# Router logits of two batches at once, with the expert vectors as weights on column groups, and routing by pairs of batches

## The chip, the core and the metric

The kernel runs on one core of one Trainium2 chip; all data is float32. The metric is the device time of one execution in microseconds (us). Engines of the core: TensorE (PE in the profile; its weight loads are listed apart as PEld), VectorE (DVE), ScalarE (ACT), GpSimd (POOL) and SyncE (SP, which only issues transfers).

## The reference, cut to what matters

One decoder layer over 16 batches of 256 tokens of width 256, in three blocks with a normalisation (mean and deviation) behind each: a gated recurrence, a cross-attention of the tokens over a context of 77 rows and themselves (8 heads of width 128), and a mixture of 8 experts.

```python
x = layernorm(x + recurrence(x))                 # 16 states per token, a scan over 256 steps
x = layernorm(x + cross_attention(ctx, x))       # keys: 77 of ctx + 256 of x = 333
x = layernorm(x + experts(x))

def experts(x):
    dot = x.reshape(4096, 256) @ expert_embeddings.T         # 4096 x 8 logits
    vals, idx = top_k(dot, 2)                                # two experts a token
    weights = softmax(dot at idx, -inf elsewhere)
    ones = weights > 0
    cap_ones = where(cumsum(ones, axis=0) <= 512, ones, 0)   # 512 places an expert, in token order
    vals, index = top_k((weights * cap_ones).T, 512)         # each expert's tokens
    inter = relu(x[index] @ first_linear.T)
    out = inter @ second_linear.T * vals
    return zeros.at[index].add(out)
```

The counting runs in token order, so a batch is placed after all batches before it: a running count by expert (`carry`) goes from batch to batch.

## The kernel before

**The loop.** The main part is a loop over 16 batches x 8 heads. Every head has the same work on TensorE: keys `pk` and queries `pq` (`head_kq`), the scores `s` (`head_softmax`), the turn of the normalised weights `pa`, `pb` (`head_turn`), and the product with the values `po` (`head_out`, two heads later). In between, each head carries steps of other stages, by a schedule written out by hand: `at(b, h, f)` puts a step behind `head_kq` of batch b, head h, and `behind(b, h, f)` puts it behind the turn of the head before. A rule of the order: within one pass the order is `head_kq`, the steps of `at`, `head_out` of two heads ago, `head_softmax`, `head_turn` of one head ago, the steps of `behind`. Each engine executes its instructions in the order in which the program gives them, unless a tile waits for a buffer; an `issue_after` pushes instructions behind a named one.

**What rides on batch b for the batch before.** While batch b's heads run, batch b-1 is finished:

- heads 1 to 3: the output projection, in two parts. `project_sums` makes sums of head outputs (`osum`, `ot`; the last of them on VectorE, L708 and L709) and `project_pairs` multiplies them (`pw`, L729). Part 0 also makes `xb`, the tokens plus a bias, on GpSimd (L722), with an `issue_after` on the power `normed[b + 2]` of a later batch's normalisation. Part 1 ends in the second normalisation, whose powers GpSimd computes (L136).
- head 5: `turn_tokens` turns the 256 finished tokens into `x2` (256 features in two blocks of 128 partitions by 256 tokens), one buffer.
- head 6: `score_experts` (L819) multiplies: for each of the two blocks of tokens and of features one instruction with 128 columns of `x2` as weights and the 8 expert vectors `emb_s` as the moving side, four products, each of which is two records of the trace (`pl`, eight records in all); each writes 8 columns. A copy takes the logits to `lg`.
- head 6: `choose`, some twenty small VectorE operations on tiles of 128 x 2 x 8: the first and second maximum, their one-hot masks, the two weights, and `on`, the mask of chosen experts. The columns behind each token (`xs[:, :, 256:262]`: weights, token number, slots) are written here and in `dispatch`, the token numbers by GpSimd.
- head 7: `dispatch`: `pc` (L886, L887), two products of `on` with a triangle and with ones, which count tokens by expert; then the places (`base`, `cum`, `place`) and the row indices `sidx` (L918); then four indirect transfers (L921, issued by GpSimd) scatter the 2 x 128 token rows with two choices each to `xg` in device memory.
- head 7: `settle`, the normalisation of the tokens as they are without any expert, and a store of them.

**What rides on batch b for the next one.** For an even next batch, made in pairs, the recurrence: `rec_state` at (3, 0), (7, 0), (11, 0) takes four batches at once. Each of the four fills 32 rows of one result tile: `px` (L360, 32 weight columns, 256 wide, four blocks of the inner width for each of the four column groups, 32 records) and `sg` (L372), then `zb` on VectorE (L380), exponentials on ScalarE, a product `pp` with a permutation (L385), and the scan on VectorE; `rec_add` (`py`, L404) one head later needs the scan. `rec_out` normalises and writes `xs`. For every next batch `prep_norm` makes the third normalisation: GpSimd's chain `again` gives `rlz` (L136), and `zl` on VectorE (L500) applies it; `prep_keys`, `prep_sums`, `prep_values` follow.

**Softmax.** `nm` (L604, the row maximum), two exponentials into `p`, `rs` (L610, the reciprocal of the sum), then `pn` = `p` times `rs` into a tile of its own (L613); the turn reads `pn`.

**The tail.** After the last head, batch 15's projection, routing and scatters, then the experts in slots, one behind the other: rows of an expert's tokens are read (`xe`), turned (`turn_rows`, `pe`, L1143), multiplied by the first matrix (`pi`, L1158) and by the second one (`pf`, L1183, four tiles of 128 tokens). In the loop over the slots, `turn_rows` of the next slot stands ahead of `second_product` of this one, except for slot 0.

```python
            at(b, 5 - early, turn_tokens, b - 1)
            at(b, 6 - early, score_experts, b - 1)
            at(b, 6 - early, choose, b - 1)
            at(b, 7 - early, dispatch, b - 1)
            at(b, 7, settle, b - 1)
```

(`early` is 2 in the last batch and 0 elsewhere.)

## Time and profile before

| what | value |
|---|---|
| median of three runs | 1172.68 us (1170.93 to 1177.48) |
| the profiled execution: its time | 1174.61 us |
| its span, first to last instruction | 1172.9 us |
| mean granted clock of TensorE | 0.998 |
| scatters of the router, GpSimd L921 | 64 of 1.03 us each |
| count of logit records `pl` | 8 a batch, in 16 batches |
| value products `po`, the largest group of TensorE | 768 of 0.38 us, 190.9 us in all |
| largest group of VectorE, the row maximum `nm` | 128 of 0.85 us, 108.3 us in all |

The profile is of one execution. Its time is that of the device, and its span goes from the first to the last instruction; 1.7 us lie around the span. "Busy" is the time in which an engine executed something; matmuls are pipelined and their ends are modelled, so on TensorE the distance from one start to the next one is a better price than the listed duration. In a row of a group, `out<-in` names the tiles, `x8` the number of instructions put together, and what stands in brackets is the idle time ahead of it and who ended it. In a slice of 40 equal parts each is 29.3 us long:

```profile
PE   7999999999999999999999999999999999999996
...
POOL 2211243113311331232213322232122212144454
PEclk9999999999999999999999999999999999999999
```

TensorE is short of 9 tenths in the first slice and in the last one alone, and at full granted clock all along. GpSimd is at 1 to 4 tenths up to the tail.

### The profile page before, as it was taken

The page shows a single profiled execution, that of the slowest core. Times are in us where ns is not written, and L with a number is a line of the kernel's source. Part 1 is how long each engine was busy: PE and PEld are TensorE (multiplying, and loading weights), DVE is VectorE, ACT ScalarE, POOL GpSimd, SP SyncE. Part 2 cuts the span into 40 slices and gives each one's busy share as a digit, 9 for nine tenths or more (in the row PEclk, how much of TensorE's full clock was granted, in tenths as well). Part 3 has the DMA queues.
Part 4 walks back from the last instruction along what each step waited for, and adds up shares of the span by engine and source line. Part 5 has one row for each costly group of instructions (what it writes and reads, how often), then busy time and mean ns, then how long its engine had stood idle before and what let it go on. Part 6 is the DMA issues. An engine that isn't in the chain of part 4 may idle for free. (4 is left out here: it accounts for less than half of the span.)

```text
span 1172.9 us, 16419 instructions
## 1 busy us (share of the span) xinstructions
PE 1140.7 (97%) x5436; PEld 833.5 (71%) x5436; DVE 812.1 (69%) x2367; ACT 494.5 (42%) x1298; POOL 321.2 (27%) x564
## 2 busy tenths in 40 slices
PE   7999999999999999999999999999999999999996
PEld 3465676777787877677777777687877778876664
DVE  6655878686757776876678767766576664665665
ACT  3344444443444444444445444444444443523331
POOL 2211243113311331232213322232122212144454
PEclk9999999999999999999999999999999999999999
DMA  7740101001000010000000100000001000045752
GB/s 253 217 144 33 35 22 37 12 28 39 24 25 17 28 37 22 27 29 19 15 10 24 37 14 10 14 19 14 10 14 46 24 10 12 21 162 137 180 161 87
DMA packets 47149, 60.67 MB, mean 52 GB/s; under 512 B 7941, under 2 KB 37102, under 8 KB 47064
## 3 DMA queue, kind: packets, MB, share of 16 engines
q1 hardware_dynamic: 39686, 50.31, 13.5%
q0 software_dynamic: 6048, 9.22, 3.1%
q8 instruction: 43, 0.70, 0.3%
q14 instruction: 42, 0.34, 0.1%
q10 hardware_dynamic: 1330, 0.10, 0.1%
HBM read 36.33 MB, written 30.78 MB: 57 GB/s over the span
## 5 line engine op out<-in xcount | busy, mean ns | idle before, releaser
L639 PE MATMUL po<-ptt,v 128*128 128x256 f32 (+1 forms) x768 | 190.9, 382 | 1.6 <-DVE rs L610 1.6
L639 PEld LDWEIGHTS po<-ptt,v 128*128 128x128 f32 (+1 forms) x768 | 141.5, 190 | 53.1 <-issue 35.5
L587 PE MATMUL pk<-kvt,wkv_s 128*128 128x333 f32 x512 | 165.3, 444 | 0.0
L602 PE MATMUL s<-kt,qt 128*128 128x333 f32 x512 | 164.3, 442 | 0.0
L604 DVE TENSOR_REDUCE nm<-s 128x2 f32<-128x666 f32 x128 | 108.3, 846 | 54.3 <-PE s L602 54.1
L608 ACT ACTIVATE p<-s,nm 128x333 f32<-128x333 f32 x256 | 135.4, 535 | 22.6 <-DVE nm L604 21.9
L647 ACT ACTIVATE ot<-po,bkv_s 128x256 f32<-128x256 f32 x128 | 60.8, 475 | 172.0 <-PE po L639 171.0
L592 PE MATMUL pq<-kvt,wq_s 128*128 128x256 f32 x512 | 131.2, 379 | 0.0
L587 PEld LDWEIGHTS pk<-kvt,wkv_s 128*128 128x128 f32 x512 | 91.1, 191 | 45.9 <-issue 23.2
L602 PEld LDWEIGHTS s<-kt,qt 128*128 128x128 f32 x512 | 96.5, 189 | 30.9 <-issue 0.5
L592 PEld LDWEIGHTS pq<-kvt,wq_s 128*128 128x128 f32 x512 | 96.7, 189 | 30.5 <-issue 0.5
L628 ACT COPY ptt<-pb 77x256 f32<-77x256 f32 x128 | 47.2, 369 | 163.1 <-PE pb L625 163.1
L613 DVE TENSOR_SCALAR pn<-p,rs 128x333 f32<-128x333 f32 x256 | 100.8, 429 | 3.3
L921 POOL DMA_INDIRECT xg<-xs,sidx x64 | 65.6, 1025 | 89.2 <-DVE sidx L918 58.5
L627 DVE COPY ptt<-pa 128x512 f32<-128x512 f32 x128 | 87.2, 682 | 0.6 <-PE pa L625 0.6
L625 PEld LDWEIGHTS pa<-ident,pn 128*128 128x128 f32 x512 | 63.9, 141 | 29.3
L589 ACT ACTIVATE kt<-pk,bkv_s 128x333 f32<-128x333 f32 x128 | 68.9, 538 | 24.6 <-PE pk L587 23.8
L625 PE MATMUL pa<-ident,pn 128*128 128x128 f32 x512 | 76.8, 273 | 0.0
L339 DVE SCALAR_TENSOR_TENSOR cv<-hp,cw,cv 128x512 f32<-128x512 f32 (+1 forms) x108 | 73.9, 691 | 1.4
L594 ACT ACTIVATE qt<-pq,bqs 128x256 f32<-128x256 f32 x128 | 61.0, 477 | 18.8 <-PE pq L592 14.9
L324 PE MATMUL ph<-xT,inw 128*128 128x512 f32 (+1 forms) x144 | 63.4, 570 | 5.0 <-DMA inw<-in_in_wT 4.9
L1183 PE MATMUL pf<-w,it 128*128 128x256 f32 x272 | 61.3, 381 | 2.7 <-ACT ye L1193 1.5
(254 smaller groups left out, 1826.8 us busy)
## 6 DMA issues: line engine op xcount, KB each, us to landing
v<-vc SPq DMA_DIRECT2D x16, 308.0 KB
xg<-zero SPq DMA_DIRECT2D x34, 131.0 KB
xe<-xg SPq DMA_DIRECT2D x8, 524.0 KB
xt<-in_x_in SPq DMA_DIRECT2D x16, 256.0 KB
out<-o SPq DMA_DIRECT2D x16, 256.0 KB
w<-in_w1T SPq DMA_DIRECT2D x8, 512.0 KB
w<-in_w2T SPq DMA_DIRECT2D x8, 512.0 KB
oe<-ye SPq DMA_DIRECT2D x15, 256.0 KB
```

Of the source, the lines that this page charges most:

```text
L339: V.scalar_tensor_tensor(cv, hp[:, :, k : k + S], cw[:, c, k : k + 1], cv, ALU.mult, ALU.add)
L587: T.matmul(pk[:, 0:J], lhsT=wkv_s[:, k, f], rhs=kvt[:, k, :], start=(k == 0), stop=(k == DC - 1))
L589: A.activation(kt, pk[:, 0:J], AF.Identity, bias=bkv_s[:, h : h + 1])
L592: T.matmul(pq[:, 0:S], lhsT=wq_s[:, k, f], rhs=kvt[:, k, 0:S], start=(k == 0), stop=(k == DC - 1))
L602: T.matmul(s[:, ic, 0:J], lhsT=qt[:, ic * P : (ic + 1) * P], rhs=kt, start=True, stop=True)
L604: V.tensor_reduce(nm, s[:, :, 0:J], AX.X, ALU.max, negate=True)
L608: A.activation(p[:, ic, :], s[:, ic, 0:J], AF.Exp, bias=nm[:, ic : ic + 1], accum_out=sm[:, ic : ic + 1])
L613: V.tensor_scalar(pn[:, ic, :], p[:, ic, :], rs[:, ic : ic + 1], None, ALU.mult)
L625: T.transpose(dst[0:jn, c0 : c0 + P], pn[:, ic, j0 : j0 + jn], ident)
L627: turned = V.tensor_copy(ptt[:, 0:2, :], pt01.rearrange("p (j i) -> p j i", j=2))
L639: T.matmul(po[:, 0:S], lhsT=vs[b][0:jn, jc, h * DH : (h + 1) * DH], rhs=ptt[0:jn, jc, :], start=(jc == 0), stop=(jc == 2),)
L921: dma = G.indirect_dma_start(out=xg[:, :], out_offset=bass.IndirectOffsetOnAxis(ap=sidx[:, t, c : c + 1], axis=0), in_=xs[b][:, t, :], in_ ...
```

## The change

Fourteen of sixteen batches, 0 to 13, are now routed in pairs (0, 1), (2, 3), ... (12, 13). Batches 14 and 15 are routed singly as before.

- **Logits.** The tokens of both batches stay turned in `x2` (now two buffers). At an even batch b, head 6, `score_pair(b - 2)` uses the expert vectors as weights, padded with zeros to 32 columns, and the 256 tokens as the moving side: four products, one for each batch and each half of the features, each to a column group of its own, so to 32 of the 128 rows of one result tile. ScalarE copies it out as `lt`. The two halves of the features are not yet summed. `turn_logits`, behind head 6's turn, multiplies `lt` (as weights, 128 tokens at a time) by `sel`, a constant mask of 128 x 16 that adds the two halves and sorts by batch and expert: 16 columns a block of tokens. A copy brings them to `lg`.
- **Routing.** `choose(b - 2, 2)` stands behind head 6 and `dispatch(b - 2, 2)` behind head 7, on tiles of 128 x 4 x 8, one chain for two batches; tags that had two buffers have one. What follows each token is written to a small tile `know`, and ScalarE copies it behind the tokens, one copy a batch. `pc` is one pair of products with 32 columns.
- **Scatters.** `dispatch` scatters the first batch's four; `scatter_second`, in the next, odd batch (3 to 13) behind head 1 and with an `issue_after` on `normed` of a later batch, the second batch's four. The last pair (12, 13) scatters all at once.
- **The recurrence.** `rec_state` is cut: `px`, `sg`, `zb` and the exponentials stay, and `rec_scan` with `pp` and the scan goes to a new place, `amid`, between `head_out` and `head_softmax` of the same head.
- **Softmax.** The weights are normalised in place; `p` has three buffers.
- **The tail.** In slot 1 one tile of `second_product` goes ahead of `turn_rows(2)`.
- **Small ones.** `yl` and the two context ends use the buffer of `osum`; one of the context's value tiles moves with `x2`; an early Tanh on two columns; six buffers of `xs` for five.

```diff
-    xpool = ctx.enter_context(tc.tile_pool(name="x", bufs=5))
+    xpool = ctx.enter_context(tc.tile_pool(name="x", bufs=6))
...
-    emb_s = wpool.tile([P, DC, E], F32, tag="emb", name="emb_s")
+    emb_s = wpool.tile([P, DC, 32], F32, tag="emb", name="emb_s")
+    sel = wpool.tile([P, 2, E], F32, tag="sel", name="sel")
...
+    A.activation(small.tile([P, 2], F32, tag="warm", bufs=1, name="warm"), nhalf, AF.Tanh)
...
+        G.memset(emb_s[:, :, E:], 0.0)
+        id5 = ident.rearrange("p (i k s) -> p i k s", k=DC, s=32)
+        V.tensor_tensor(sel, id5[:, :, 0, 0:E], id5[:, :, 1, 0:E], ALU.add)
...
         A.activation(dec[R], dec[R], AF.Exp, scale=-1.0)
+        scans[first] = R, rows, members, sg, zb, dec
+        if first == 0:
+            rec_scan(first)
+    def rec_scan(first):
+        R, rows, members, sg, zb, dec = scans.pop(first)
         pp = bank(f"pp{first}")
...
-        p = b2.tile([P, 2, J], F32, tag="p", name=f"p{b}_{h}")
+        p = b2.tile([P, 2, J], F32, tag="p", bufs=3, name=f"p{b}_{h}")
...
-            V.tensor_scalar(pn[:, ic, :], p[:, ic, :], rs[:, ic : ic + 1], None, ALU.mult)
+            V.tensor_scalar(p[:, ic, :], p[:, ic, :], rs[:, ic : ic + 1], None, ALU.mult)
...
-        x2s[b] = b1.tile([P, DC, S], F32, tag="x2", name=f"x2{b}")
+        x2s[b] = b2.tile([P, DC, S], F32, tag="x2", name=f"x2{b}")
...
+    def score_pair(b):
+        pl = bank(f"pl{b}")
+        for k in range(DC):
+            for i in range(2):
+                r = 32 * (DC * i + k)
+                T.matmul(pl[r : r + 32, 0:S], lhsT=emb_s[:, k, :], rhs=x2s[b + i][:, k, :], start=True, stop=True)
+        del x2s[b], x2s[b + 1]
+        logits[b] = lt = b1.tile([P, S], F32, tag="lt", name=f"lt{b}")
+        A.copy(lt, pl[:, 0:S])
+    def turn_logits(b):
+        lt = logits.pop(b)
+        pt = bank(f"plt{b}")
+        for t in range(GT):
+            T.matmul(
+                pt[:, t * 2 * E : (t + 1) * 2 * E],
+                lhsT=lt[:, t * P : (t + 1) * P],
+                rhs=sel.rearrange("p i e -> p (i e)"),
+                start=True,
+                stop=True,
+            )
+        lgs[b] = small.tile([P, 2 * GT, E], F32, tag="lg", bufs=1, name=f"lg{b}")
+        V.tensor_copy(
+            lgs[b].rearrange("p (i t) e -> p t i e", t=GT),
+            pt[:, 0 : 2 * GT * E].rearrange("p (t i e) -> p t i e", i=2, e=E),
+        )
...
-        for i in range(GT):
-            G.tensor_scalar(x[:, i, D + 2 : D + 3], tok1, float(b * S + i * P), 1.0, ALU.add, ALU.mult)
+        x = small.tile([P, 2 * GT, DX - D], F32, tag="know", bufs=1, name=f"know{b}")[:, 0:TT, :]
+        for i in range(TT):
+            G.tensor_scalar(x[:, i, 2:3], tok1, float(b * S + i * P), 1.0, ALU.add, ALU.mult)
...
-        T.matmul(pc[:, 0 : GT * E], lhsT=tri, rhs=onf, start=True, stop=True)
-        T.matmul(pc[:, GT * E : 2 * GT * E], lhsT=ones, rhs=onf, start=True, stop=True)
+        T.matmul(pc[:, 0 : TT * E], lhsT=tri, rhs=onf, start=True, stop=True)
+        T.matmul(pc[:, TT * E : 2 * TT * E], lhsT=ones, rhs=onf, start=True, stop=True)
...
-        for t in range(GT):
+        for i in range(n):
+            A.copy(xs[b + i][:, :, D:], x[:, i * GT : (i + 1) * GT, :])
+        scatter(b, sidx, range(GT if b + 4 < B else TT))
+        sidxs[b] = sidx
+    def scatter_second(b):
+        with tc.issue_after(normed[b + 4].ins):
+            scatter(b, sidxs[b], range(GT, 2 * GT))
+    def scatter(b, sidx, tiles):
+        for t in tiles:
             for c in range(2):
                 dma = G.indirect_dma_start(
...
+    def amid(b, h, f, *args):
+        mid_steps[b, h].append((f, args))
...
-            at(b, 6 - early, score_experts, b - 1)
-            at(b, 6 - early, choose, b - 1)
-            at(b, 7 - early, dispatch, b - 1)
+            if b == B - 1:
+                at(b, 6 - early, score_experts, b - 1)
+                at(b, 6 - early, choose, b - 1, 1)
+                at(b, 7 - early, dispatch, b - 1, 1)
+            elif b % 2 == 0:
+                at(b, 6, score_pair, b - 2)
+                behind(b, 6, turn_logits, b - 2)
+                behind(b, 6, choose, b - 2, 2)
+                behind(b, 7, dispatch, b - 2, 2)
+            if b % 2 == 1 and 2 < b < B - 1:
+                behind(b, 1, scatter_second, b - 3)
...
                 at(b, 0, rec_state, nb, nb + 3)
+                amid(b, 0, rec_scan, nb)
...
         if i >= 2:
             head_out(*heads[i - 2])
+        if i < len(heads):
+            for f, args in mid_steps[heads[i]]:
+                f(*args)
...
-            if e > 0:
-                turn_rows(e + 1)
-        y = second_product(e, it)
+        tiles = list(range(SLOTS[e][2]))
+        ahead = 1 if e == 1 else 0
+        if ahead:
+            second_product(e, it, tiles[:ahead])
+        if 0 < e < LAST:
+            turn_rows(e + 1)
+        y = second_product(e, it, tiles[ahead:])
```

## The prediction

> **What bounds the kernel now.** I read the page first: TensorE is the bound.
>
> ```profile
> PE 1140.7 (97%) x5436; PEld 833.5 (71%) x5436; DVE 812.1 (69%) x2367; ACT 494.5 (42%) x1298; POOL 321.2 (27%) x564
> ```
>
> An instruction taken off TensorE is therefore worth its time, and one taken off VectorE is worth nothing unless TensorE waits for it. So the second view is who TensorE waited for (total us, times, longest).
>
> ```profile
> PE pp L385 <- issue: 3.9, 3, 1.3
> PE po L639 <- DVE rs L610: 1.6, 1, 1.6
> PE pe L1143 <- DMA xe<-xg: 1.6, 1, 1.6
> ```
>
> The first and third row are waits that the change reaches for; the second it leaves alone. Third, the timeline of TensorE where batch 3 is routed (start, us, then the group; a row's price is the distance to the next row's start).
>
> ```profile
> 367.28 0.95 PE L819 MATMUL pl<-emb_s,x 128*128 128x8 f32 x8
> 368.09 1.10 PE L552 MATMUL pv<-wsum,tsum 128*128 128x512 f32 x2
> ...
> 374.95 0.37 PE L886 MATMUL pc<-on,tri 128*128 128x16 f32 x2
> 375.17 0.37 PE L887 MATMUL pc<-on,ones 128*128 128x16 f32 x2
> 375.39 1.96 PE L324 MATMUL ph<-xT,inw 128*128 128x512 f32 x4
> ```
>
> The logits take 0.81 us and the two count products 0.44, although they write 8 and 16 columns. The matmuls behind run 0.08 over their usual time (1.10 for two `pv`, 1.02 elsewhere). One batch costs 0.89 + 0.52 = 1.41.
>
> **Off TensorE: logits and counts by pairs.** Fourteen batches are routed by pairs, two as before. A pair costs 2.82 now. Afterwards it has one pair of count products (four instructions, 0.52), one turn of the same form (128 weight columns, 16 written: 0.52), and eight instructions of 32 weight columns by 256 on four column groups. This last form the trace shows in the recurrence, at 262.98 us:
>
> ```profile
> 262.98 1.93 PE L360 MATMUL px<-hs,xpw 128*32 128x256 f32 x32
> 264.73 0.61 PE L372 MATMUL sg<-sums,half 128*32 128x256 f32 x8
> 265.27 0.70 PE L639 MATMUL po<-ptt,v 128*128 128x256 f32 x2
> 267.31 0.70 PE L385 MATMUL pp<-zb,perm 128*128 128x256 f32 x2 [1.34 <-issue]
> 267.85 1.03 PE L639 MATMUL po<-ptt,v 128*128 128x256 f32 x4
> 268.72 1.28 PE L602 MATMUL s<-kt,qt 128*128 128x333 f32 x4
> ```
>
> and on VectorE, whose `zb` reads `px`:
>
> ```profile
> 266.77 0.48 DVE L380 TENSOR_SCALAR zb<-px,xpb 128x256 f32<-128x256 f32 x1 [2.62 <-PE po L639]
> ```
>
> Forty of them are issued in 265.27 - 262.98 = 2.29 us, 0.057 each, against 0.216 for the same width on the whole array (1.73 us for eight `pf` of L1183). But `zb` starts at 266.77, 1.86 after the end that is modelled for `px` (264.91): by its reader, 32 took 3.79, 0.118 each. Eight cost 0.46 by the issue, 0.95 by the reader, 1.73 if nothing overlapped. Entering and leaving the form costs 0.1 each (four `pq` before `px` take 0.96 to the next start, 0.86 before `pc`; two `po` behind show 0.70, not 0.60). The pair then costs 1.70, 2.19 or 2.97; the gain over seven pairs is 7.8, 4.4 or a loss of 1.1. I take the middle of the first two, **-6.1**: the matmuls behind did start on time, but the wait at `pp` may hide what was still running. All three ends stay for the range.
>
> A rule speaks against this edit. "TensorEngine Tiling (Array Packing)" of the Trainium skill, section Performance Considerations, says that a matmul has some 60 cycles of overhead, so that free size 1 costs what 60 costs, and warns against tiling for a dimension that is already small. An estimate by that page (60 cycles at the 2.4 GHz of "TensorE: Matmul & The Clock Gate") gives 0.025 us for each old logit product, 0.4 a pair, and the sum would be 8.5 us worse. The rows have 0.10 each, with their 128-column weight loads, so the measurement decides for the edit.
>
> **VectorE.** Each pair runs one chain of some 36 small operations for two, on 32 instead of 16 elements, at about 0.2 us each in both forms (0.17 in the rows of 16). That saves about 25 us of VectorE and is worth 0 directly: no routing operation of VectorE stands among TensorE's longest waits. The in-place softmax, the third buffer of `p`, the early Tanh (one table load at 5.26, as before) and the moved constants cost nothing; the idle time of ScalarE (42% busy) covers its seven copies of 128x256 (0.37 each, as the 77x256 copy of L628) and sixteen narrow ones. Without that cover they would cost about 5 us.
>
> **`pp` moved behind `po`.** At three places (batches 3, 7, 11) four `po` instructions go ahead of `pp`: 268.72 - 267.85 = 0.87 saved if TensorE was idle, 0 if it was still finishing `px`. I take half, **-1.3** (0 to -2.6). What is late next is the scan: it now stands behind a row maximum and a copy (0.76 + 0.68) on VectorE, and `py` needs it. Its slack now is 272.57 - 271.43 = 1.14, so about 0.3 each, **+1.0** (0 to 3.5).
>
> **The late pair chain at the same three places.** `pc` now stands ahead of `px`, behind `pq` of the next batch's head 0, and its input `on` stands behind `rs` of the last head. `rs` is at 263.26 and `pq` ends its issue at 262.98; with `on` and its landing `pc` can start about 0.5 after TensorE asks for it: **+1.5** (0 to 2). Behind it stand `px` and everything else.
>
> **One product of expert slot 1 ahead of the turn.** Eight `pf` (1.73 us) fill the wait of 1.64 for the rows of `xe`: **-1.6** (0 to -1.6). The turned rows still have 1.73 of `pf` to cover their eviction.
>
> **The scatters in two parts.** The built order on GpSimd is: first four scatters, four token operations, `ra`, second four, `xb`, and only then `uz`, `u2z`, `u3z`, `rlz`, which `zl` waits for. On VectorE `zl` stands ahead of L708, whose result the second half of `pw` needs. These six odd batches (3 to 13) now look like batch 3:
>
> ```profile
> 265.94 0.97 POOL L921 DMA_INDIRECT xg<-xs,sidx  x1 [0.30 <-issue]
> 267.22 0.98 POOL L921 DMA_INDIRECT xg<-xs,sidx  x1 [0.30 <-issue]
> 277.12 0.72 POOL L136 TENSOR_TENSOR ra<-va,nhalf 128x2 f32<-128x2 f32 x1 [8.93 <-DVE va L147]
> 277.83 1.37 POOL L722 TENSOR_TENSOR xb<-xs,bo_s 128x256 f32<-128x256 f32 x2
> ...
> 280.05 1.07 POOL L136 TENSOR_TENSOR rlz<-u3z,nhalf 128x2 f32<-128x2 f32 x1
> ```
>
> ```profile
> 281.15 0.35 DVE L500 TENSOR_SCALAR zl<-xs,rlz 128x256 f32<-128x256 f32 x1 [0.52 <-POOL rlz L136]
> ...
> 282.28 0.69 DVE L708 TENSOR_TENSOR ot<-osum,ot 128x512 f32<-128x512 f32 x1
> ```
>
> ```profile
> 286.67 1.05 PE L729 MATMUL pw<-wosum,ot 128*128 128x128 f32 x8
> ```
>
> A scatter takes 1.28 of GpSimd (265.94 to 267.22), four 5.1. They push `rlz` from 281.12 to 286.2; two `zl` (0.65) and L708 (0.69) end at 287.6, where TensorE wants it at 286.67: a wait of about 1.0. Batches 5, 9 and 13 have a second one: the first four scatters wait for the later chain, and with the token operations (four, some 1.1) and a sum (1.3) they end about 0.4 after `ra` is due. 6 x 1.0 + 3 x 0.4 = **+7.2** (0 if `zl` is not in the way, 12 if it is 2.0 each time). The old scatters at the end of every batch cost TensorE nothing, so removing those saves nothing.
>
> **Sum.** -6.1 - 1.3 + 1.0 + 1.5 - 1.6 + 7.2 = +0.7. The profiled execution had a span of 1172.9 and a time of 1174.6, so it would come to 1175.3; it lies 1.9 above the median of the runs, 1172.7, and on the median's footing this is **1173.4**: no change that can be told.
>
> **Rivals.** *The second scatters stay hidden* (chance 0.25): -6.1 - 1.3 + 1.0 + 1.5 - 1.6 = -6.5, 1166.2. For it: 5.5 us lie between the first `rlz` and the second half of `pw`. Against: `zl` and L708 use those up by the built order. *GpSimd becomes the bound of every odd batch* (0.22), the slower one: the place is `ra` behind the first four scatters. It decides once `sidx` comes so late that they end after `ra` is due (in batch 5, after 393.45, which is `sidx` later than about 387). From there each us counts at `pw`'s first half as well; at 2.5 a batch it is 15 in place of 7.2, +8.5, 1181.2. For it: the pair's chain comes a head later. Against: batches 3, 7 and 11 have 5 us of room. *The column groups do not overlap* (0.05): +1.1 for -6.1, +7.9, 1180.6. The issue of `px` speaks against it, its reader half for it.
>
> **How the numbers follow.** About 0.5%, 5.9 us, is what a measurement of this kernel can tell from no change. The forecast holds 0.48 (its own range 1168 to 1178), faster by more 0.25, slower by more 0.27. To leave out no more than 2 in 10 the range takes in most of both sides: low is 1165 (the full issue rate, 1.7 better, with the hidden scatters), high 1181 (GpSimd late).
>
> **What would show it.** In the changed trace: `pl` in rows of 128x256 with about 0.06 between starts and `lt` copied 0.5 us after the last; TensorE's wait list with `pw <- DVE` at odd batches from 3 to 13, some 1 us each, and none in even ones; `pc` waiting for `on` at three places; no wait of `pe` for `xe`; `pp` at under 3.9. I am wrong if `pw` shows no waits (then 1166) or if `ra` is late by over a us in each odd batch.

## The result, and the profile after

| | before | after |
|---|---|---|
| median of 20 runs each | 1172.74 us (1170.61 to 1177.65) | 1169.95 us (1166.52 to 1172.19) |
| ratio of the medians, 95% interval | | 0.9969 [0.9959, 0.9978] |
| the profiled execution: time, span | 1174.61, 1172.9 us | 1172.19, 1170.5 us |
| start to the first `s` | 51.41 | 52.80 |
| batch 0 | 82.59 | 82.89 |
| the loop, batch 1 head 0 to batch 15 head 7 | 883.63 | 879.39 |
| from there to the end (the tail) | 155.27 | 155.39 |

The kernel became 0.3% faster. That is clear of the interval of its measurement, although it is less than the 0.5% which the prediction took for the least that can be told; 1173.4, no change, had been forecast. The last four rows are distances between the starts of `s` (the scores) in the two traces. The loop is what can be compared: a second profile of the changed kernel, on chip 13, had it at 879.37. Start and tail move by some microseconds from one execution to the next (50.6 to 54.8 and 149.8 to 157.3 in the profiles of this study), so most of what follows is read from the loop. It lost 4.24 us.

From the page of the kernel after, the busy times and the row of GpSimd in 40 slices:

```profile
PE 1136.3 (97%) x5380; PEld 822.2 (70%) x5380; DVE 782.1 (67%) x2144; ACT 497.1 (42%) x1315; POOL 318.0 (27%) x565
...
POOL 3201241114210530242015302340142014144454
```

TensorE has 56 matmuls and 4.4 us of work less, VectorE 30.0 us less (the prediction had about 25), and the time moved by 2.4 in the profiles. GpSimd has the same work, but in heaps: slices of 4 and 5 tenths beside slices of 0, where it lay between 1 and 4 before, and nowhere at 0. The heaps are the odd batches with eight scatters.

Who TensorE waited for, after (total us, times, longest):

```profile
PE pw L745 <- DVE ot L724: 3.5, 6, 1.3
...
PE pw L745 <- DVE ot L721: 1.9, 3, 0.7
PE pi L1239 <- issue: 1.7, 1, 1.7
...
PE pc L936 <- DVE on L926: 1.6, 3, 0.5
...
PE pe L1224 <- DMA xe<-xg: 0.3, 1, 0.3
```

`pw` and `pc` wait where they were said to (the longest of the three waits for L721, 0.7, is at batch 1 and stood in the kernel before too). `pe` has almost no wait left, but `pi`, behind it, has a new one of the same length. And a line is missing: before, `pp <- issue` stood there with 3.9, three times 1.3.

The timeline of the kernel after at the same place (batch 3, head 0), TensorE and then VectorE:

```profile
263.46 0.38 PE L936 MATMUL pc<-on,tri 128*128 128x32 f32 x2 [0.54 <-DVE on L926]
...
264.00 1.93 PE L368 MATMUL px<-hs,xpw 128*32 128x256 f32 x32
265.75 0.61 PE L380 MATMUL sg<-sums,half 128*32 128x256 f32 x8
266.29 1.56 PE L655 MATMUL po<-ptt,v 128*128 128x256 f32 x6
267.69 0.60 PE L402 MATMUL pp<-zb,perm 128*128 128x256 f32 x2
```

```profile
266.16 0.35 DVE L969 SCALAR_TENSOR_TENSOR sidx<-into,oobs,know 128x4 int32<-128x4 f32 x2
266.43 0.48 DVE L388 TENSOR_SCALAR zb<-px,xpb 128x256 f32<-128x256 f32 x1
```

`zb` starts 2.43 after the first `px`, and directly behind `sidx`, so it was VectorE that kept it. Before, the same `zb` started 3.79 after `px` with VectorE idle for 2.62 us. The matmuls are the same 32 records. Something that made `px` look slow is gone; whether that is the place of `pp`, the experiments have to tell.

Step by step, from the starts of `s` head by head (after minus before):

| step | forecast | measured |
|---|---|---|
| logits and counts by pairs, seven pairs | -6.1 | -7.9: 1.34 to 1.41 less in each odd batch and 0.13 to 0.27 less in each even one at heads 6 and 7, 0.45 more for `pc` in the head behind; so a pair costs some 1.69 in place of 2.82 |
| wait of `pp` at batches 3, 7, 11, and the later `py` | -1.3 + 1.0 | -4.6 and 0 |
| `pc` waits for `on` | +1.5 | +1.6 |
| scatters in two parts, `pw` waits | +7.2 | +6.85: batch 3 0.47, 5 2.43, 7 0.44, 9 2.41, 11 0.43, 13 0.67 |
| one product ahead in slot 1 (tail) | -1.6 | +0.5 up to the first `pi` of slot 2 |

The four rows of the loop give -4.05, against -4.24 measured; the rest is in batch 1 (0.10 more at its first head, 0.23 less at its last).

### The profile page after: what moved, and what is told of

Its sections match the earlier page's. It is cut to its first block, busy times and chain, and to the rows that moved or that the text cites. A ratio compares the mean times of both kernels' runs of the same rounds, so it can differ in the third digit from the quotient of the medians.

```text
span 1170.5 us, 16021 instructions
## 1 busy us (share of the span) xinstructions
PE 1136.3 (97%) x5380; PEld 822.2 (70%) x5380; DVE 782.1 (67%) x2144; ACT 497.1 (42%) x1315; POOL 318.0 (27%) x565
## 5 line engine op out<-in xcount | busy, mean ns | idle before, releaser
L629 DVE TENSOR_SCALAR p<-p,rs 128x333 f32<-128x333 f32 x256 | 98.3, 420 | 3.3
L641 PEld LDWEIGHTS pa<-ident,p 128*128 128x128 f32 x512 | 63.9, 141 | 29.4
L641 PE MATMUL pa<-ident,p 128*128 128x128 f32 x512 | 76.8, 273 | 0.0
```

Source lines behind the costliest of these rows:

```text
L629: V.tensor_scalar(p[:, ic, :], p[:, ic, :], rs[:, ic : ic + 1], None, ALU.mult)
L641: T.transpose(dst[0:jn, c0 : c0 + P], pn[:, ic, j0 : j0 + jn], ident)
```

## The experiments

Theories that had to be told apart: is the lost wait at `pp` worth what `pp`'s move brought, or did `px` itself become prompt, and why? Is the pair's form really cheaper than the old one? What does the late scatter cost, what the product ahead? The kernel before was run again beside each set. The runs went to several chips, and its median was 1174.3 us on chip 4, 1175.2 on chips 13 and 1, 1166.9 on chip 8 and 1166.5 on chip 6; ratios are against the runs on the same chip. "Loop" is the loop of the table above, 883.63 before and 879.39 after.

**`pp` and the scan moved alone, in the kernel before.**

```diff
+        scans[first] = R, rows, members, sg, zb, dec
+    def rec_scan(first):
+        R, rows, members, sg, zb, dec = scans.pop(first)
         pp = bank(f"pp{first}")
...
                 at(b, 0, rec_state, nb, nb + 3)
+                amid(b, 0, rec_scan, nb)
```

> The kernel before with one edit: `rec_scan` (`pp` and the scan) goes behind `head_out`, so that all six `po` stand ahead of `pp` at batches 3, 7 and 11. Theory A (an idle TensorE keeps back the signal of `px`, so the whole wait goes): `zb` starts about 2.4 us after `px` as in the changed kernel, not 3.79 as before; TensorE's wait at `pp` (3.9 in all) goes, about 1.4 a place, 4.2 in all: 0.9964 of before, about 1168.5. Theory B (as predicted: `px` is still being finished, the wait only overlaps four `po`): `zb` stays at 3.79 after `px`, some 0.4 of wait is left at each `pp`, 0.43 to 0.87 gained a place, and `py` waits 0.3: 0 to 2.6 in all, about 1172.

1175.84 us, 1.0014 [1.0001, 1.0028]; loop 884.47, 0.84 longer. Who TensorE waited for in it:

```profile
PE py L413 <- DVE ys L401: 3.1, 3, 1.0
...
PE pp L394 <- issue: 1.3, 3, 0.5
```

The move does what the prediction said, with a wrong balance: each place gains 0.89 at `pp` and loses 1.25 at `py`, where the prediction had 0.43 and 0.3 (and 0.09 to 0.14 comes back one head later). `zb` still comes 3.78 after `px`, with VectorE idle.

**The kernel after, with `pp` and the scan back in their old place.**

```diff
-        if first == 0:
-            rec_scan(first)
+        rec_scan(first)
...
-                amid(b, 0, rec_scan, nb)
```

> The changed kernel with `rec_scan` put back into `rec_state`, so that `pp` follows two `po` again; `pc` still stands ahead of `px`. Theory A: `zb` goes back to 3.8 us after `px` and `pp` waits 1.3 at three places: 4.2 slower than the changed kernel, about 1174.2. Theory B: the place of `pp` is worth 0.3 in all, about 1170.3. Theory C (it is the wait for `pc` ahead of `px` that makes `px` early, not the place of `pp`): `zb` stays at about 2.4 after `px`, `pp` waits some 0.2 at each place, 0.6 in all, about 1170.6.

1171.30 us, 0.9973 [0.9956, 0.9991]; loop 879.34, the same as after. `zb` comes 2.44 after `px`, and no wait of `pp` is among TensorE's. So the place of `pp` is worth nothing in the kernel after, and the 4.6 us come from a prompt `px`.

**The kernel after, with the old form of logits for each pair** (sixteen records with 128 weight columns, no `turn_logits`).

```diff
-                at(b, 6, score_pair, b - 2)
-                behind(b, 6, turn_logits, b - 2)
+                at(b, 6, score_both, b - 2)
```

> The changed kernel with the logits of a pair in the form of before: tokens as weights, 8 columns written, sixteen records a pair, no column groups, no turn, no copy to `lt`. Everything else by pairs. Theory A (column groups overlap at their issue rate, as the changed trace shows: the step at head 6 costs 0.77 and the turn 0.44): a pair of logits costs 1.62 + 0.16 in place of 1.21, 0.57 more, 7 pairs: 4.0 slower than the changed kernel, about 1174.0. Theory B (they cost by the rate that the reader of `px` showed, 0.95 + 0.1 + 0.52): 1.78 in place of 1.57, 1.5 slower, about 1171.4. In both `on` comes earlier and `pc` waits less at batches 3, 7 and 11, up to 1.5 to be taken off.

1174.98 us, 0.9999 [0.9989, 1.001]; loop 882.0, 2.6 longer than after. Logits in the kernel after, then in this one (TensorE and the copies):

```profile
247.99 0.64 PE L854 MATMUL pl<-x,emb_s 128*32 128x256 f32 x8
248.56 1.13 PE L569 MATMUL pv<-wsum,tsum 128*128 128x512 f32 x2
249.07 0.38 ACT L857 COPY lt<-pl 128x256 f32<-128x256 f32 x1
```

```profile
248.77 1.85 PE L854 MATMUL pl<-emb_s,x 128*128 128x8 f32 x16
250.47 1.10 PE L569 MATMUL pv<-wsum,tsum 128*128 128x512 f32 x2
```

Eight records on the column groups take 0.57 to the next start and are read 1.08 after the first; sixteen in the old form take 1.70. From the starts of `s` the old form costs 0.93 to 1.02 more a pair and saves the turn, 0.45; so the new form is 0.48 to 0.57 a pair better, 3.7 over seven, of which this run gets some 1.1 back because the counts come earlier and `pc` needn't wait. Here `px` stands directly behind `pq`, as in the kernel before, and `zb` is still prompt (2.00 after `px`): so it is not the `pc` between `pq` and `px` that made it so.

**The scatters beside `px` taken away, in the kernel before.** The four scatters of batches 1, 5 and 9 get their indices from a copy that is made behind `zb`; nothing else is changed.

```diff
+        if b not in (1, 5, 9):
+            scatter(b)
+    def scatter_late(b):
+        late = small.tile([P, GT, 2], I32, tag="late_idx", bufs=1, name=f"late_idx{b}")
+        with tc.issue_after(zbs[b + 3].ins):
+            V.tensor_copy(late, sidxs[b])
+        sidxs[b] = late
+        scatter(b)
...
                 at(b, 0, rec_state, nb, nb + 3)
+                behind(b, 0, scatter_late, b - 2)
```

> The kernel before, with the four scatters of batches 1, 5 and 9 held back until `zb` of the recurrence is done (a copy of their indices on VectorE behind `zb`, 0.16 us, is what they wait for); no other edit, `pp` stays where it was. Theory D (scatters that GpSimd issues while the forty column-group products run are what makes `px` late: in before they start at 263.24 and 504.41, 0.26 and 0.25 after `px`; in the changed kernel and its variants none runs there and `px` is signalled 0.04 after its end): `zb` starts about 2.0 after `px` instead of 3.8, the wait of 1.3 at `pp` goes at three places: 3.9 to 4.5 faster than before, 0.9964. Theory E (the cause is another difference, such as where the tiles lie): `zb` stays at 3.8 after `px`, 0 to 0.5.

1169.71 us, 0.995 [0.9932, 0.9969]; loop 878.48, 5.15 shorter than before: 1.73, 1.66 and 1.71 at batches 3, 7 and 11. Its timeline at batch 3, TensorE, VectorE and GpSimd:

```profile
265.88 1.93 PE L360 MATMUL px<-hs,xpw 128*32 128x256 f32 x32
...
267.88 0.48 DVE L380 TENSOR_SCALAR zb<-px,xpb 128x256 f32<-128x256 f32 x1 [0.83 <-PE px L360]
...
268.71 0.59 PE L385 MATMUL pp<-zb,perm 128*128 128x256 f32 x2
...
268.73 1.12 POOL L937 DMA_INDIRECT xg<-xs,late_idx  x1 [5.94 <-DVE late_idx L929]
```

`zb` comes 2.00 after `px`, at the end that is modelled for it, and `pp` waits for nothing. This one edit, which takes no work from any engine, gains as much as the whole change; its loop, 878.48, is even 0.9 shorter than that of the kernel after, so everything else in the change together costs 0.9 in the loop.

**More scatters beside `px`, in the kernel after.** Four more at the same three places, to rows that nothing reads (work that is added to the kernel).

```diff
+        where = small.tile([P, 4], I32, tag="where", bufs=1, name=f"where{b}")
+        with tc.issue_after(on_ins[b].ins):
+            V.tensor_copy(where, rows_i[:, b : b + 4])
+            for t in range(4):
+                dma = G.indirect_dma_start(
+                    out=nowhere[:, :],
...
                 behind(b, 7, dispatch, b - 2, 2)
+                if b in (2, 6, 10):
+                    behind(b, 7, scatter_more, b - 2)
```

> The changed kernel with four more scatters on GpSimd at batches 3, 7 and 11, of the token columns of a finished pair to rows that nobody reads, issued some 0.3 us after the start of `px`. Theory D: the signal of `px` is late again, by about 1.8, and `zb` starts some 3.8 after `px` and not 2.4 to 2.7; `pp`, which has four more `po` ahead of it than in before, waits 0.4, and `py` about 1.0 for the scan as in the run with `pp` moved alone; 1.2 to 1.5 a place, 4 in all. The real first scatters come 5 us later, which the 2.9 to 5 us up to `ra` hide at these batches or miss by up to 1. Theory E: `px` stays at 0.04, and only the late scatters can cost, 0 to 3 in all.

1192.40 us, 1.0147 [1.0129, 1.0166]; loop 897.12, 17.7 longer than after (3.9, 6.7 and 7.2 at the three places). At batch 7:

```profile
508.29 1.93 PE L368 MATMUL px<-hs,xpw 128*32 128x256 f32 x32
508.93 1.13 POOL L986 DMA_INDIRECT nowhere<-xs,where  x1 [5.20 <-DVE base L942]
...
513.35 0.48 DVE L388 TENSOR_SCALAR zb<-px,xpb 128x256 f32<-128x256 f32 x1 [2.29 <-PE po L655]
513.89 0.46 PEld L402 LDWEIGHTS pp<-zb,perm 128*128 128x128 f32 x2 [2.14 <-DVE zb L388]
```

The same `px` is now read 5.06 after its start, with VectorE idle for 2.29 and TensorE waiting for the answer. The direction was expected, the size wasn't: other matmuls' results (`po`, `pp`) are late as well, and at batches 7 and 11 the granted clock then stood at 0.50 for 3.4 us, behind idle stretches of TensorE of 1.74 and 3.47; at batch 3, where the run lost least, it did not fall.

**Which part of a scatter does it?** In the kernel after, at the same three places, seven elementwise operations of 128x256 on GpSimd in one run, and eight plain transfers of 128 KB issued by SyncE in another (added work in both).

```diff
+            G.tensor_scalar(junk, xs[b][:, t % 2, 0:D], tick[:, 0:1], 1.0, ALU.mult, ALU.mult)
```

```diff
+            nc.sync.dma_start(nowhere[r : r + P, :], rows_)
```

> The changed kernel with seven elementwise operations of 128x256 on GpSimd beside `px` at batches 3, 7 and 11 (their results are read by nobody), where k11 had four scatters. If GpSimd's being busy is what delays the signals, `px` is signalled 1 to 2 us after its end and `zb` starts 3.5 or more after `px`, as in k11. If it is the transfers or their indirect issue, the signal stays at 0.04 and `zb` at 2.4 to 2.7. The real scatters come later by some 5 us, up to 2 in all.

> The changed kernel with eight plain transfers of 128 rows of 1 KB from the on-chip memory to rows that nobody reads, issued by SyncE beside `px` at batches 3, 7 and 11: as many bytes as eight scatters without GpSimd. If moving the rows is what delays the signals, `px` is signalled 1 us late or more. If it is the indirect issue on GpSimd, the signal stays at 0.04 and `zb` at 2.4 to 2.7 after `px`: no change of time.

1171.54 and 1171.22 us, one execution each, on chip 1; loops 879.76 and 879.49 against 879.39. The end of `px` is signalled within 0.05 us of the modelled end in both, as without them; `zb` comes 2.85 and 2.0 to 2.1 after `px` (2.85 because VectorE is busy with `sidx`). So neither these operations on GpSimd nor this plain traffic to device memory does it, on a chip where signals near scatters are late. What in an indirect scatter does is open.

**The second scatters held behind the last power of the chain (`rlz`).**

```diff
-        with tc.issue_after(normed[b + 4].ins):
+        with tc.issue_after(zpower[b + 4].ins):
...
-                behind(b, 1, scatter_second, b - 3)
+                behind(b, 4, scatter_second, b - 3)
```

(`zpower` names the instruction that writes `rlz`.)

> The changed kernel with the second four scatters of a pair pushed behind `rlz` on GpSimd. Theory A (they stand ahead of `rlz`, and `zl` holds L724 back on VectorE): the waits of `pw` part 2 go (0.45, 1.55, 0.44, 1.55, 0.43 and 0.67 at batches 3 to 13, 5.1 in all), those of part 1 at batches 5 and 9 (0.86 each, from the first four) stay: about 1164.9. Rival (GpSimd's 5.1 us a pair only move to the sums `tsum` behind it, and `pv` waits in their place): no change, about 1170.

1167.11 us, 0.9933 [0.9915, 0.995]; loop 875.75, 3.64 shorter than after. Three waits of `pw` for the earlier sum (L721 in the kernel after) are left, 3.4 in all in place of 1.9: at batches 5 and 9 they became 0.7 longer, which is why the gain is 3.64 and not 5.1.

**All eight scatters behind `rlz`.** `dispatch` keeps `sidx`, and `scatter_second` issues all eight.

```diff
-        scatter(b, sidx, range(GT if b + 4 < B else TT))
+        if b + 4 >= B:
+            scatter(b, sidx, range(TT))
...
-            scatter(b, sidxs[b], range(GT, 2 * GT))
+            scatter(b, sidxs[b], range(2 * GT))
```

> The changed kernel with all eight scatters of a pair pushed behind `rlz` on GpSimd. Theory A: all waits of `pw` at odd batches go, 5.1 in part 2 and 1.7 in part 1 (batches 5 and 9), 6.9 in all: about 1163.1. Rival: 10.2 us of scatters ahead of `tsum` on GpSimd make `pv` wait for the sums at odd batches; from then on each us costs six times, and the gain over moving the second four alone (1.7) is lost.

1163.05 us, 0.9965 [0.9952, 0.9977] on chip 8; loop 873.9, 5.5 shorter than after. `pw` keeps 1.5 of its waits: 0.7 at batch 1, which the kernel before has too, and 0.4 each at batches 5 and 9. So 5.5 of the 6.85 belong to the place of the scatters. What stays at batches 5 and 9 (0.65 each from the starts of `s`) does not.

**No product ahead in slot 1.**

```diff
-        ahead = 1 if e == 1 else 0
+        ahead = 0
```

> The changed kernel without the tile of `second_product` ahead of `turn_rows(2)` in slot 1. Theory A (the step gained nothing: the wait for `xe`, 1.6, became one for `xet`, 1.7, since VectorE evicts the turned rows behind 26 small operations): the wait of `pe` comes back, that of `pi` goes, 0.1 either way, about 1170. Theory B (as predicted, a gain of 1.6): about 1171.6.

1169.92 us, 1.0026 [1.0017, 1.0036] on chip 8. `pe` waits 2.2 for its rows. Then `pe` and half of `pf` run slowly. Stretches of the tail: us from to, length, then busy time and instructions of five engines, the granted clock of TensorE, the share of the DMA engines and GB/s:

```profile
1047.00:1049.70 2.70, 0.52 (x3) 0.12 (x1) 1.27 (x6) 0.46 (x2) 2.38 (x3) 1.00 0.93 273
1049.70:1051.50 1.80, 1.76 (x9) 1.77 (x9) 1.65 (x14) 0.00 (x0) 1.06 (x2) 0.52 1.01 300
1051.50:1053.00 1.50, 1.50 (x5) 1.23 (x5) 1.47 (x13) 0.59 (x1) 1.04 (x2) 0.50 1.07 388
```

The clock fell to half for some 3 us after an idle stretch of 2.2 us. In the kernel before the wait was 1.64 and the clock stayed full. So the product ahead is worth 1.9 here (first `pi` of slot 2 at 40.7 us behind the last head, against 38.8), but by keeping the clock: from the first `pe` to that `pi` it is 6.06 here and was 4.39 in the kernel before, for the same work. Against the kernel before (38.2) it is worth nothing.

**The turned rows copied first.** The reads of the next slots' small data are held behind the copies of `xet`.

```diff
-                V.tensor_copy(xet[:, k, 0 : n * P], pt[:, 0 : n * P])
+                turned_rows[e] = V.tensor_copy(xet[:, k, 0 : n * P], pt[:, 0 : n * P])
...
+        if e == 1:
+            with tc.issue_after(turned_rows[2].ins):
+                rows[2].read(2)
```

> The changed kernel, with VectorE's copy of the turned rows of slot 2 put ahead of the small operations on the rows of slots 2 and 3 (`dw` to `to`), by their order alone. Theory A (the copy at 1053.04 is late because of them; the transposes end at 1050.4): the copy starts at about 1050.7 of the same scale, the wait of `pi` (1.7) goes: 1.7 faster than the changed kernel, about 1168.3. Rival (ScalarE's half of the copy or the small operations become late in their turn): 0 to 0.5.

1166.38 us, 0.9997 [0.9984, 1.001] on chip 8. The tail of the kernel after, and then of this one:

```profile
1049.33 1.09 PE L1224 MATMUL pe<-ident,xe 128*128 128x128 f32 x8 [0.32 <-DMA xe<-xg]
1050.26 1.89 PE L1266 MATMUL pf<-w,it 128*128 128x256 f32 x8
1053.83 5.39 PE L1239 MATMUL pi<-xet,w 128*128 128x512 f32 x12 [1.68 <-issue]
```

```profile
1049.96 1.09 PE L1226 MATMUL pe<-ident,xe 128*128 128x128 f32 x8 [0.83 <-DMA xe<-xg]
1050.89 1.89 PE L1268 MATMUL pf<-w,it 128*128 128x256 f32 x8
1052.62 3.69 PE L1241 MATMUL pi<-xet,w 128*128 128x512 f32 x8
```

After, VectorE did 26 small operations from 1050.21 on ahead of the copy `xet` (1053.04), and `pi` waited 1.68. With the copy first `pi` waits for nothing and starts at 37.5 in place of 38.8, which is 0.7 better than before.

**Both of these together,** all eight late and the copy first.

> Both mends together: all eight scatters behind `rlz`, and the copy of the turned rows first. If both theories hold the gains add, 6.9 + 1.7 below the changed kernel: about 1161.4, 0.990 of before. If either falls, what the single runs show.

On chip 8 1159.37 us, 0.9941 [0.9925, 0.9958]; loop 873.89. On chip 1 the same kernel:

> The best version (all scatters behind `rlz`, copy of the turned rows first) again. From the profiles it should stand 5.5 (scatters) + 1.4 (copy) below the changed kernel, whose ratio was 0.9957 to 0.9969: 0.990 to 0.992.

1173.31 us, 0.9986 [0.9976, 0.9995]; loop 882.68, 8.8 longer. The same place of batch 3 in the two runs, the end of the second half of `pw` and its reader on VectorE, on chip 8 and then on chip 1:

```profile
286.18 0.97 POOL L989 DMA_INDIRECT xg<-xs,sidx  x1 [0.30 <-issue]
...
286.60 1.06 PE L748 MATMUL pw<-wosum,ot 128*128 128x128 f32 x8
287.45 0.97 POOL L989 DMA_INDIRECT xg<-xs,sidx  x1 [0.30 <-issue]
287.69 0.29 DVE L765 TENSOR_TENSOR u<-u,pw 128x128 f32<-128x128 f32 x1 [2.94 <-PE pw L748]
```

```profile
288.39 0.97 POOL L989 DMA_INDIRECT xg<-xs,sidx  x1 [0.30 <-issue]
...
288.82 1.06 PE L748 MATMUL pw<-wosum,ot 128*128 128x128 f32 x8
289.67 0.97 POOL L989 DMA_INDIRECT xg<-xs,sidx  x1 [0.30 <-issue]
...
292.10 0.29 DVE L765 TENSOR_TENSOR u<-u,pw 128x128 f32<-128x128 f32 x1 [5.14 <-PE po L658]
```

The eight scatters run at the same place in both. On chip 8 VectorE reads `pw` 1.09 after the last group began, on chip 1 3.28 after. That delay reaches `ptt` and six `po` (7.0 us of waits there, at head 4 of the odd batches). So whether a scatter holds a signal back differs between the two runs of one kernel, and moving the scatters away from `px` put them beside `pw`. Each chip was used for one set of runs, so the chip and what else differed between the sets can't be told apart.

**Counts one head later** (both late, and `dispatch` behind the next head's turn).

```diff
-                behind(b, 7, dispatch, b - 2, 2)
+                behind(b + 1, 0, dispatch, b - 2, 2) if b < B - 2 else behind(b, 7, dispatch, b - 2, 2)
```

> The best version so far (all scatters behind `rlz`, copy of the turned rows first) with `dispatch` of a pair one head later, behind head 0 of the odd batch, so that `pc` no longer stands between `pq` and `px`. The waits of `pc` for `on` at batches 3, 7 and 11 (0.55 each, 1.6 in all) go: 1.6 faster than the best version if nothing else waits. Rival: the counting chain on VectorE, 11 operations, now stands among those of head 1 and holds back the sums for `pw` or the row maxima: the gain is lost, 0 to 1 slower.

1180.71 us, 1.0052 [1.0033, 1.0072] on chip 13; loop 888.64. It failed: `po` waits 5.2 for `ptt`, and `pw` 3.0. On chip 1, where signals are late too, the loop without the later count was 882.68; against that it is 6.0 longer. So of the 14.75 us that it is above the loop on chip 8 (873.89), some 8.8 go with late signals and some 6.0 with the later count (an estimate, since the runs are of different chips).

**Routing half a head earlier** (`score_pair` behind head 5's turn, the turn of the logits and `choose` at head 6), with both of the two, on chip 1; then the second scatters late with the copy first, on chip 6; then these with the earlier routing.

```diff
-                at(b, 6, score_pair, b - 2)
-                behind(b, 6, turn_logits, b - 2)
-                behind(b, 6, choose, b - 2, 2)
+                behind(b, 5, score_pair, b - 2)
+                at(b, 6, turn_logits, b - 2)
+                at(b, 6, choose, b - 2, 2)
```

> The best version (k8) with the routing of a pair half a head earlier: `score_pair` behind head 5, `turn_logits` and `choose` at head 6. `on` is then ready before `pc` wants it and the waits of `pc` at batches 3, 7 and 11 (0.55 each, 1.6 in all) go: 1.6 faster than k8. Rival: the 25 small operations of `choose` come into the way of `v` and `ptt` on VectorE in head 6, as the counting chain did in k10: slower by some us.

> The changed kernel with the second four scatters behind `rlz` (k4: 3.6 less in the main loop) and the copy of the turned rows first (k7: 1.4 less in the tail). No scatter then runs beside `px` or ahead of the reader of the second `pw`: about 5.0 below the changed kernel, 0.991 to 0.993 of before on a chip that holds signals back, 0.994 to 0.996 on one that does not (there the kernel before has no wait at `pp`, some 4.5 less).

> k15 with the routing of a pair half a head earlier (k14: 0.9 less in the main loop than k8, from `pc` that no longer waits). Expected another 0.9 below k15. Rival: the first scatters come earlier by about 0.7 and reach into `px`, whose signals are then held back at batches 3, 7 and 11: 2 to 4 slower than k15.

Earlier routing is worth 0.9 in the loop both times (881.8 against 882.68 on chip 1, 874.93 against 875.82 on chip 6): `pc` then waits for nothing. (The medians on chip 1, 1173.29 and 1173.31, don't show it.) Times: 1173.29 us, 0.9976 [0.996, 0.9992]; 1162.81 us, 0.9972 [0.9961, 0.9983], where 0.994 to 0.996 had been expected; 1161.51 us, 0.9953 [0.9939, 0.9966].

**The changed kernel again, on chip 13.**

> The changed kernel itself, beside the others on the same chip, since the kernel before took 1174.3 on one chip and 1166.9 on another, and so ratios of different calls can't be set against each other. If its gain is in the main loop (4.4 in the profiles, from batch 1 on, the same to 0.1 in every execution profiled) the ratio is 0.996 to 0.998 here too; a ratio above 1 would say that the start or the tail differ by chip.

1169.50 us, 0.9957 [0.9942, 0.9972]; loop 879.37 against 879.39.

The best ratios are 0.9933 (second scatters late, chip 4), 0.9941 (both late, copy first, chip 8) and 0.9953 (second late, copy first, earlier routing, chip 6). They come from different chips and can't be set against each other or against the 0.9957 and 0.9969 of the kernel after; the last arrangement wasn't run on a chip that holds signals, so which is best there is open.

## Why the prediction missed, step by step

**The step that failed** is the last sentence on the scatters: "The old scatters at the end of every batch cost TensorE nothing, so removing those saves nothing". Three of their sixteen sets ran beside `px`, and there they cost 4.6 to 5.1 us: this is what the kernel after gained at `pp`, and what the kernel before gains when only those scatters are held back. The forecast for the loop was +2.3 and the measurement is -4.24; of the difference 4.3 stand at `pp` and `py`, 1.8 at the pairs and 0.4 at the scatters. That the time still fell inside the forecast's own 1168 to 1178 is luck: the largest gain came from a cause that the sum put at nothing.

It could have been seen in the profile of before. The prediction priced `px` "by its reader" at 0.118 a record from the one row where `zb` is late. The trace has another `px`, at 129.29 us, with no scatter near (TensorE, then VectorE):

```profile
129.29 1.92 PE L360 MATMUL px<-hs,xpw 128*32 128x256 f32 x16
...
131.37 0.46 DVE L380 TENSOR_SCALAR zb<-px,xpb 64x256 f32<-64x256 f32 x1
```

Here the reader starts 2.08 after `px`, 0.16 behind its modelled end; at batch 3 it started 3.79 after, 1.86 behind the end. (This `px` uses two column groups and that of batch 3 four, so it is a hint and no proof.) The first scatter of batch 3 starts 0.26 behind `px`:

```profile
263.24 1.13 POOL L921 DMA_INDIRECT xg<-xs,sidx  x1 [3.35 <-DVE into L917]
```

**The pairs** (-6.1, measured -7.9): right in kind, and mis-sized by the same error. The middle of "0.46 by the issue, 0.95 by the reader" was taken; the full issue rate holds, and a pair costs 1.69, the low end of the prediction (1.70). The 1.41 of each odd batch came out as 1.34 to 1.41. The decision to trust the rows and not the estimate of 0.025 us for an old product was right: sixteen of them take 1.70 here, and going back to them costs 3.7 over seven pairs.

**`pp` behind `po`** (-1.3) **and `py`** (+1.0): in the kernel after worth 0 and 0, since nothing was late any more. Alone, in the kernel before, -2.7 and +3.75. What 0.89 saved at `pp` does to `py` was left out: TensorE comes there 0.89 sooner, so the slack of 1.14 shrinks to 0.25, and a scan that is 1.44 later costs 1.19 in place of 0.3 (1.25 measured).

**The wait of `pc`** (+1.5): 1.6, three times 0.5, as said.

**The scatters in two parts** (+7.2): 6.85. The mechanism of the wait in the second half of `pw` is in the timeline of the kernel after at batch 5, GpSimd, VectorE and TensorE:

```profile
393.83 0.72 POOL L136 TENSOR_TENSOR ra<-va,nhalf 128x2 f32<-128x2 f32 x1 [0.67 <-DVE va L147]
...
398.95 0.97 POOL L985 DMA_INDIRECT xg<-xs,sidx  x1 [0.30 <-issue]
...
402.05 0.72 POOL L136 TENSOR_TENSOR rlz<-u3z,nhalf 128x2 f32<-128x2 f32 x1
...
402.80 0.61 DVE L517 TENSOR_SCALAR zl<-xs,rlz 128x256 f32<-128x256 f32 x2 [5.28 <-POOL rlz L136]
...
403.33 0.68 DVE L724 TENSOR_TENSOR ot<-osum,ot 128x512 f32<-128x512 f32 x1
...
404.07 0.97 PEld L745 LDWEIGHTS pw<-wosum,ot 128*128 128x128 f32 x8 [1.67 <-DVE ot L724]
```

`pw` stands behind `ot`, that behind `zl`, that behind `rlz`, and `rlz` behind the last scatter. That the sum comes so close is partly luck, since the distribution differs from the forecast: 0.45 in place of 1.0 at batches 3, 7 and 11, 2.4 in place of 1.4 at 5 and 9, and 0.67 in place of 1.4 at 13. The second term, `ra` kept late by the first scatters, did not happen: at batch 5 GpSimd is idle for 0.67 ahead of `ra` and waits for `va` of VectorE. What makes the first half of `pw` wait there (0.89) is VectorE, which reaches `osum` 4.36 behind the start of `py` in place of 3.51 before; with all eight scatters moved it is 4.31. That the pair's counting chain ahead of it is the reason is likely, but not shown. Held behind `rlz`, the second scatters give back 3.64, all eight 5.5.

**The product ahead** (-1.6): +0.5, of which 0.4 is that the rows `xe` came later behind the last head in this execution; from the first `pe` to the first `pi` it is 4.50 in place of 4.39. The wait for `xe` went as said, from 1.64 to 0.32. What failed is "The turned rows still have 1.73 of `pf` to cover their eviction": 26 operations stand ahead of the eviction on VectorE, and the cover of sixteen `pf` (3.46 us) that the kernel before had behind its `pe` had been cut to eight. With the copy first the gain is 0.7.

**The rivals.** Scatters that stay hidden are ruled out by the waits, GpSimd as the bound of every odd batch too (at most 2.43, and in two batches of six), and column groups that don't overlap by the 1.69. What happened was no rival of the list: the gain of the edit came from moving work that had no visible price.

**Chips.** The late `px` of the kernel before was seen in its own profile and on chip 4 (in the run that moves `pp` alone), and on chip 13 the kernel gains by holding the scatters back. On chips 8 and 6 no signal of TensorE was late near a scatter, and there the kernel before takes 1166.5 to 1166.9 us, 7 to 9 less. The change with its tail mended (copy first) is worth nothing on chip 8 (0.9997), where its gain on the pairs (7.9) is used up by the waits that it adds (1.6 and 6.85). That the kernel before has no wait at `pp` there was not profiled; it is inferred from its time and from the late signals below, and `px` explains 4.6 to 5.1 of the 7 to 9; the rest is open. The kernel after doesn't depend on it: its loop is 879.34 and 879.38 on chip 8, in the two kernels that differ from it in the tail alone.

## What to carry to other kernels

Before a stretch is priced by when its reader starts, look for the same instruction elsewhere in the trace: where one place is 1.8 us later than its twins, ask what ran beside it and not what it is. An operation that is off the critical path and shares no data with it can still cost time by where it runs, so work that is moved counts at its old place as well as at its new one. And a filler that goes ahead of a waiting instruction takes its cover from whatever comes next: list what stands between the next result and its reader on the other engine.

## What the runs showed of the hardware that was not expected

- **Results of TensorE are reported late while an indirect scatter runs,** on some chips. Counted in the loop are the signals of TensorE of which none came within 0.2 us behind the modelled end; "near" is within 0.5 us of a scatter on GpSimd. Near a scatter it was 19 of 100 before and 35 of 103 after, elsewhere 0 of 879 and 0 of 866. On chips 4, 13 and 1 it was 18 to 43 of 86 to 112 near scatters in twelve runs (0 to 4 of some 870 elsewhere); on chips 8 and 6 it was 0 of 86 to 117 in six runs. Some such entries may be records that the trace lost; the readers that start late (`zb`, `u`) are the proof. At batch 3 of the kernel before the next recorded signal behind `px`, `sg` and the `po` that follows them is one and the same, 1.84, 1.41 and 0.78 behind their modelled ends, as if they had been held and let go together; in the run with more scatters that of `px` was 1.6 to 3.1 late. Whether the results themselves were late, or only their signals, the traces don't tell.
- **Half the clock after a short idle.** An idle stretch of 2.22 us in the tail was followed by 3.4 us at a granted clock of 0.50, and one of 1.64 was not. The length of the one stretch does not decide it: in the run with more scatters one of 1.74 was followed by half the clock, and near the start of the run with plain transfers one of 2.51 was not. The Trainium skill ("TensorE: Matmul & The Clock Gate", Part 1) states half rate after an idle window of about 3.4 us; here shorter stretches were enough.
- **Column groups run at their issue rate.** Eight records of 32 weight columns by 256 take 0.57 to the next start, and 32 are done when their modelled end says so.
- **The loop repeats to 0.05 us** (879.39 and 879.37 in two profiles of the kernel after, 879.34 and 879.38 on chip 8 with other tails), while start and tail vary by 4 and 7 us: comparing starts of one repeated instruction tells apart steps that the medians can't.
